# Router's weights loaded first, last feed-forward's norms ahead of its products, last layer's pairs of spread values in one buffer and placed together

## The chip, the cores and the metric

The kernel runs on one core of a Trainium2 chip. The metric is the device time of one execution in microseconds (us). TensorE (PE in the profile), VectorE (DVE), ScalarE (ACT), GpSimd (POOL) and the DMA queues issued by SyncE (SP) and POOL each take their instructions strictly in the order that the program gives them.

## What is computed

A residual stream x of 4 batches x 1024 tokens x 128 channels (f32) passes four layers. Each is a half feed-forward, an attention of some kind, and the same half feed-forward again. The norms have no weights.

```python
x = x + 0.5 * moe0(ln(x));  x = x + attn0(ln(x));  x = x + 0.5 * moe0(ln(x))      # 8 experts, top 2, gelu
x = x + 0.5 * ffn1(ln(x));  x = x + attn1(ln(x));  x = x + 0.5 * ffn1(ln(x))      # silu-gated; 16 heads of 8, rotary
x = x + 0.5 * moe2(ln(x));  x = x + attn2(ln(x));  x = x + 0.5 * moe2(ln(x))      # 8 experts, relu; linear attention
x = x + 0.5 * ffn3(ln(x));  x = x + attn3(ln(x));  x = x + 0.5 * ffn3(ln(x))
# attn3 (16 heads of 8), by token t:   y = r_t . (S + u * k_t v_t);   S = S * exp(-exp(w_t)) + k_t v_t
```

## The kernel before, in words

Channels are the partitions, so the residual of a batch is one 128 x 1024 tile X. All products are f32; a matmul of this type is two PE instructions, so x2 in the trace is one matmul. Nearly all of them go through the helper `mm` (L231).

**Order of the work.** The code states tasks, and a scheduler fixes each engine's order when the program is built, by priority (order of statement, unless raised) and by its own estimate of when operands and buffers are free. `lanes` states several tasks side by side: each task yields its estimated cost, and the lane with the lowest clock goes on. In layer 1's attention PE's order is written out by hand. A pool hands out buffers by tag; a new tile in a buffer waits until the old one has been read.

**Start.** `run` loads constants c0 and the four X tiles by SP's queue, then the weights named in `needs`: l0s (the router, 128 x 8), l0a (attention 0), l1f (whose integers VectorE converts at L604), then those of later layers. `run` multiplies the router's weights by a centring matrix and puts them beside that matrix in `both`, so that one matmul of X with `both` gives the centred tokens and their router logits. `layer0` then centres attention 0's q, k, v weights (`centered`, L263: one matmul, one copy on ScalarE). `route` (L306 to L432) takes squares of the centred tokens on ScalarE, norms them, and ranks, counts and places the tokens; `experts` (L450 to L483) then goes through blocks of 128 slots: fetch an expert's weights, gather tokens, two products, scatter. `combine` (L508 to L517) adds the results to X.

**Layer 1's attention** (`l1_attn`). `prepare(b)` norms a batch, makes q and k with their rotation (L712, L715, summed on POOL at L717) and v (L723); `spread` moves heads by DMA (L731) and POOL (L732) to where the products read them. The loop goes through 256 units; in each, `greatest` (products, then maxima at L744 on VectorE) runs 11 units ahead of `scores` (exponentials at L767 on ScalarE) and `values`. Layer 1's first feed-forward of batch 3 is late: `feed` does it in two halves of 512 tokens, each of 8 steps (centre and square L825, variance L833, scaling L839, three gate/up products L844 and L847, a pause, output), and one step is taken at each yield of `prepare(0)` from the third on, then one in each unit of the loop. ScalarE's square root, exponential and silu are in different tables, whose change is an ACT_TABLE_LOAD.

**Layer 3** (`layer3`). For batches (0, 1) and then (2, 3), two halves of 512 tokens each: `l3_ffn`, `l3_prepare`, `l3_recur`, `l3_finish`, `l3_ffn`, 8 units in all, in five lanes: recurrences, two lanes of finishing work, two of preparing work. The recurrence keeps state element (head, k) by partition and goes through the 8 value columns j in 4 pairs. For each pair two matmuls (tile `wave`, via `together`, L1079) spread the value rows over the partitions; they read different groups of 32 rows (32*128 in the trace). VectorE multiplies by k (`kv`, L1170), scans with the decay (`st`, L1177) and multiplies by r (`z`, L1184; the second of a pair does this on POOL). After two pairs, four matmuls (tile `acc`, also L1079) sum z over the partitions; the first set is stated after the third pair. `l3_prepare` has two pairs of mixing matmuls per unit that go through `together` as well (tile `bank` in L1079). `together` states the matmuls last to first, and a dependency without a semaphore keeps that order on PE; it does not keep other matmuls out from between:

```python
        for out, lhsT, rhs, start, stop in reversed(matmuls):
            i = self.nc.tensor.matmul(out, lhsT, rhs, start=start, stop=stop).ins
            if after is not None:
                self.tc.add_manual_dep(i, after.name, order, reason="side by side")
            after = i
```

Each `wave` tile is 128 x 512 f32, and its pool holds two of them.

Of the kernel before, what the change touches and what calls it, by code (L numbers as in the profile page):

```python
# [17 lines left out]
P = 128  # L18
B, S, D = 4, 1024, 128
# [3 lines left out]
HALF = 512  # L23
# [186 lines left out]
class Macaron:  # L210
# [449 lines left out]
    def l1_attn(self, m, c1, f):  # L660
# [6 lines left out]
        with ExitStack() as ctx:  # L667
            enter = ctx.enter_context
# [186 lines left out]
            late = [feed(b, hf) for b in self.late for hf in range(2)]  # L855
            for n, _ in enumerate(prepare(0)):
                if late and n >= 2:
                    next(late[0], None)
            for z in va:
                nc.gpsimd.memset(z, 0.0)  # L860
                nc.gpsimd.memset(z[:, :, :, 0:1], 1.0)
# [212 lines left out]

    def together(self, matmuls, after=None):

        order = mybir.DependencyInfo(mybir.DependencyClass.NoSync, mybir.DependencyReason.DATA)
        for out, lhsT, rhs, start, stop in reversed(matmuls):
            i = self.nc.tensor.matmul(out, lhsT, rhs, start=start, stop=stop).ins  # L1079
            if after is not None:  # L1080
                self.tc.add_manual_dep(i, after.name, order, reason="side by side")
            after = i
        return after
# [65 lines left out]
    def l3_recur(self, wave, ps, wp, c3, b, h, carries, given):  # L1149
        nc = self.nc  # L1150
        v, pool = nc.vector, nc.gpsimd
        wdec, k, vals, r, y = (given[x] for x in ("wdec", "k", "vals", "r", "y"))
        acc = self.t(ps, [P, HALF], "acc")
        carry = carries[b] if h else self.t(wp, [P, HD], f"carry{b % 2}")
        carries[b] = carry
        held = []
        for w in range(2):
            zs = []
            for pair in range(2):
                js = [4 * w + 2 * pair + i for i in range(2)]  # L1160
                vb = [self.t(wave, [P, HALF], "wave") for _ in js]
                rows = [slice(32 * (j % 4), 32 * (j % 4) + 32) for j in js]
                last = self.together([(vb[i], c3["vrows"][rows[i], w, :], vals[rows[i], :], True, True) for i in range(2)])
                for sums in held:
                    self.together(sums, last)
                held = []
                kv = []
                for i in range(2):
                    kv.append(self.t(wp, [P, HALF], "kv", bufs=3))
                    v.tensor_tensor(kv[i], k, vb[i], ALU.mult)  # L1170
                for i, j in enumerate(js):
                    st = self.t(wp, [P, HALF + 1], "st", bufs=3)
                    if h == 0:
                        v.memset(st[:, 0:1], 0.0)
                    else:
                        nc.scalar.copy(st[:, 0:1], carry[:, j : j + 1])
                    v.tensor_tensor_scan(  # L1177
                        st[:, 1:], wdec, kv[i], carry[:, j : j + 1] if h else 0.0, ALU.mult, ALU.add
                    )
                    if h == 0:  # L1180
                        nc.scalar.copy(carry[:, j : j + 1], st[:, HALF:])

                    z = self.t(wp, [P, HALF], "z", bufs=6)
                    (pool if i else v).tensor_tensor(z, st[:, 0:HALF], r, ALU.mult)  # L1184
                    zs.append(z)
                yield 4.7
            held.append([(acc[32 * q : 32 * q + 32, :], c3["sums"][:, w, :], zs[q], w == 0, w == 1) for q in range(4)])
        for sums in held:
            self.together(sums)
        v.tensor_tensor(y, y, acc, ALU.add)  # L1190
        yield 1
# [33 lines left out]
    def layer3(self, f, t, c3):  # L1225
        sb = lambda name, bufs=2, **k: self.tc.tile_pool(name=name, bufs=bufs, reuse_waits="tile", **k)
        with ExitStack() as ctx:
            enter = ctx.enter_context
            wave, accs, tail, prep = (
                enter(self.psum(name, n)) for name, n in (("l3wave", 2), ("l3acc", 1), ("l3tail", 2), ("l3prep", 3))  # L1230
            )

            tmp, *front = (enter(sb(name, side="right")) for name in ("l3tmp", "l3even", "l3odd"))
            rec, *end = (enter(sb(name)) for name in ("l3rec", "l3ends0", "l3ends1"))
            given, carries, seen = {}, {}, {}
            start = lambda f, *a: lambda: f(*a)
            units = [(b + i, h) for b in range(0, B, 2) for h in range(2) for i in range(2)]
            fronts, recs, ends = ([], []), [], ([], [])
            for b, h in units:
                u = f"{b}{h}"  # L1240
                mine = given[b, h] = {}
                wp, wend = front[b % 2], end[b % 2]
                s = [seen.setdefault((b, i), {}) for i in range(3)]
                fronts[b % 2].extend([
                    (f"ffn{u}0", (), start(self.l3_ffn, prep, tmp, wp, f, b, h, s[0])),
                    (f"prepare{u}", (), start(self.l3_prepare, prep, tmp, wp, t, c3, b, h, s[1], mine)),
                ])
                recs.append((f"recur{u}", (f"prepare{u}",), start(self.l3_recur, wave, accs, rec, c3, b, h, carries, mine)))
                ends[b % 2].extend([
                    (f"finish{u}", (f"recur{u}",), start(self.l3_finish, tail, wend, t, c3, b, h, mine)),  # L1250
                    (f"ffn{u}1", (), start(self.l3_ffn, tail, tmp, wend, f, b, h, s[2])),
                ])
            self.lanes(recs, *ends, *fronts)
# [47 lines left out]
        self.lanes(blocks, back, *more(route))  # L1301

    def layer0(self, moe, m, right, enter, ffn):
        m["wqkvc"] = self.centered(m["wqkv"], 3 * D)
        early = right.enter_context(ExitStack())
        pa, pf = enter(early, "l0a"), enter(right, "l1f0", side="left")
        side, main = self.side, self.main
        self.late = [B - 1]

        def swap():  # L1310

            early.close()
            self.l1_rings(enter(self.rings, "l1rings", 1))
            yield 0

        def more(route):
            attn = lambda b, *after: (f"middle{b}", after, lambda: self.l0_attn(side, pa, m, b))
            last = lambda b, ps: (f"last{b}", (f"combine1{b}",), ffn(pf, ps, b))
            return (
                [  # L1320
                    route(0, (0,), ps=main), route(0, (1,)), route(0, (2, 3)),
                    *[attn(b, f"combine0{b}") for b in range(B)],
                    ("swap", (), swap), *[last(b, side) for b in range(B) if b not in self.late],
                ],
                [route(1, (0, 1), "middle0", "middle1", "combine03"), route(1, (2,), "middle2"), route(1, (3,), "middle3")],
            )


        groups = [(0,), (1,), (2, 3)], [(0, 1), (2,), (3,)]
        marks = {(0, (0,)): "_1", (0, (1,)): "_2", (0, (2, 3)): "_0", (1, (0, 1)): "_0", (1, (2,)): "_1", (1, (3,)): "_2"}  # L1330
        self.macaron("l0", moe, AF.Gelu, groups, marks, more)
# [30 lines left out]
    def run(self, stages):  # L1362
        nc = self.nc
        self.X, self.ring, self.rings, self.late = [], {}, ExitStack(), []
        self.c0 = self.load("c0")
        for b in range(B):
            X = self.t(self.res, [P, S], f"x{b}")
# [9 lines left out]
            "l3": ("l3f", "l3a", "c3"),  # L1377
        }
        tags = {"l1a": "attn_w", "l3a": "attn_w", "c1": "attn_c", "c2": "attn_c", "c3": "attn_c"}
        have = {}  # L1380

        def weights(name):
            if name not in have:
                have[name] = self.l1_weights() if name == "l1f" else self.load(name, tag=tags.get(name))
            return have[name]

        sb = lambda name, bufs=2, **k: self.tc.tile_pool(name=name, bufs=bufs, reuse_waits="tile", **k)
        for n, name in enumerate(stages):
# [3 lines left out]
            if name in ("l0", "l2"):  # L1392
                with self.psum("main", 4) as self.main, self.psum("side", 4) as self.side, sb(name + "moe") as self.fp:
# [4 lines left out]
                    with ExitStack() as right:  # L1398
                        enter = lambda stack, name, bufs=2, side="right": stack.enter_context(sb(name, bufs, side=side))
                        m = dict(weights(name + "a"))  # L1400
# [55 lines left out]
```

## Time and profile before

| | |
|---|---|
| median of 3 runs | 3086.77 us (3083.92 to 3097.02) |
| the profiled execution | 3084.05 us, its span 3082.3 us |
| busy share of the span | PE 87%, DVE 59%, ACT 53%, POOL 26% |
| mean granted TensorE clock | 0.925 |
| layer 0, 0 to 849 us | PE 607 us busy, DVE 542, ACT 488, clock 0.84 |
| layer 1's attention, 849 to 1935 us | PE 1060 us busy, DVE 713, ACT 608, clock 0.99 |
| layer 1's second feed-forward and layer 2, 1935 to 2601 us | PE 584 us busy, DVE 325, ACT 329, clock 0.94 |
| layer 3, 2601 to 3082 us | PE 427 us busy, DVE 252, ACT 202, clock 0.90 |

The boundaries are read from the trace: the first square of layer 1's attention follows 849 us, its last copy of outputs starts at 1932, and layer 3's first norm follows the last combine at 2601. A clock of 1 is full speed. A wait shown in brackets behind a timeline row is the time for which the engine stood idle before it, with what released it. Each L number is a line of the kernel before.

### The profile page before, as it was taken

The numbers are of one execution on the slowest core, as the hardware profiler recorded it, in microseconds if no ns is written. First come the engines' busy times: TensorE is split into PE (matmuls) and PEld (weight loads), VectorE is DVE, ScalarE is ACT, GpSimd is POOL, SyncE is SP. The second block draws the span as 40 slices with busy tenths as digits, with TensorE's granted clock in tenths as the row PEclk, the third lists the DMA queues.
The fourth block names the chain that finished last, engine by engine and source line by source line (L and its number), as shares of the span: only waits on it lengthen the run. The fifth ranks groups of instructions, "written<-read, shape, count | busy, mean of one in ns | idle before, by whom it ended". The sixth has DMA issues, their size and how long they took to land. (4 is left out here: it accounts for less than half of the span.)

```text
span 3082.3 us, 47513 instructions
## 1 busy us (share of the span) xinstructions
PE 2677.2 (87%) x17694; PEld 1544.9 (50%) x17694; DVE 1832.5 (59%) x3215; ACT 1626.7 (53%) x3633; POOL 788.3 (26%) x732
## 2 busy tenths in 40 slices
PE   5868537778989999999999999989898987899997
PEld 5756416665643333333333333568787975343432
DVE  3586886774256776676677774362566632447554
ACT  4655425657725665566565666455454554353532
POOL 4666307553400000000000000037444563001010
PEclk8988768889989999999999999989998998899988
DMA  7766416563500000000000000048665784000000
GB/s 240 225 178 191 120 53 184 169 197 117 164 15 5 5 7 4 5 6 5 19 5 6 1 1 1 21 141 283 199 181 181 219 277 148 1 1 1 7 7 14
DMA packets 122887, 277.63 MB, mean 90 GB/s; under 512 B 18017, under 2 KB 67297, under 8 KB 122529
## 3 DMA queue, kind: packets, MB, share of 16 engines
q1 hardware_dynamic: 101792, 231.83, 24.3%
q0 software_dynamic: 20864, 42.77, 4.9%
q8 instruction: 140, 2.29, 0.3%
q14 instruction: 91, 0.74, 0.1%
HBM read 238.48 MB, written 31.85 MB: 88 GB/s over the span
## 5 line engine op out<-in xcount | busy, mean ns | idle before, releaser
L744 DVE TENSOR_REDUCE nm<-two 128x2 f32<-128x1024 f32 x512 | 626.2, 1224 | 276.1 <-PE s L231 265.1
L767 ACT ACTIVATE e<-s 128x512 f32<-128x512 f32 x1024 | 555.9, 594 | 400.6 <-PE s L231 397.5
L471 ACT ACTIVATE e_h<-bank,e_w 128x128 f32<-128x128 f32 x1304 | 450.3, 368 | 395.7 <-PE bank L231 383.9
L231 PE MATMUL s<-qm,kz 32*128 32x512 f32 x2048 | 631.8, 640 | 0.8 <-ACT e L767 0.8
L231 PE MATMUL bank<-e_x,e_w 128*128 128x128 f32 x2608 | 536.0, 309 | 91.1 <-ACT e_h L471 52.8
L231 PE MATMUL two<-kz,qz 32*128 32x512 f32 x2048 | 576.6, 645 | 20.6 <-DVE nm L744 4.2
L457 POOL DMA_INDIRECT e_xg<-rows,g_source x326 | 343.1, 1052 | 758.5 <-DVE g_l L317 349.9
L231 PEld LDWEIGHTS bank<-e_x,e_w 128*128 128x128 f32 x2608 | 409.1, 202 | 172.7 <-ACT e_h L471 97.6
L231 PE MATMUL bank<-e_w,e_h 128*128 128x128 f32 x2608 | 459.3, 292 | 20.9 <-ACT e_h L471 12.7
L483 POOL DMA_INDIRECT res<-e_y,g_target x326 | 360.4, 1105 | 255.7 <-DVE e_y L482 113.9
L231 PEld LDWEIGHTS bank<-e_w,e_h 128*128 128x128 f32 x2608 | 378.4, 202 | 44.3 <-ACT e_h L471 26.2
L231 PE MATMUL o<-e,va 128*32 128x256 f32 x4096 | 327.4, 391 | 0.1
L231 PEld LDWEIGHTS o<-e,va 128*32 128x32 f32 x4096 | 80.9, 108 | 387.9 <-issue 367.9
L231 PEld LDWEIGHTS two<-kz,qz 32*128 32x128 f32 x2048 | 153.8, 184 | 227.7 <-issue 162.7
L231 PEld LDWEIGHTS s<-qm,kz 32*128 32x128 f32 x2048 | 206.6, 183 | 11.3 <-issue 7.7
L463 DVE COPY e_x<-bank 128x128 f32<-128x128 f32 x326 | 92.7, 285 | 190.1 <-PE bank L461 170.2
L482 DVE TENSOR_TENSOR e_y<-bank,e_w 128x128 f32<-128x128 f32 x326 | 93.9, 288 | 187.6 <-PE bank L231 176.2
L732 POOL COPY va<-vd 128x256 f32<-128x256 f32 x16 | 6.7, 433 | 624.6 <-PE o L231 537.9
L1184 POOL TENSOR_TENSOR z<-st,r 128x512 f32<-128x512 f32 x32 | 46.4, 1449 | 414.2 <-DVE st L1177 343.6
L461 PE MATMUL bank<-c,e_xg 128*128 128x128 f32 x326 | 95.4, 295 | 46.2 <-DMA e_xg<-rows,g_source 39.7
L471 ACT ACT_TABLE_LOAD x53 | 68.0, 1283 | 28.4 <-PE bank L231 18.3
L461 PEld LDWEIGHTS bank<-c,e_xg 128*128 128x128 f32 x326 | 49.5, 152 | 52.4 <-DMA e_xg<-rows,g_source 36.0
(325 smaller groups left out, 3440.1 us busy)
## 6 DMA issues: line engine op xcount, KB each, us to landing
e_w<-in_l0m_dram SPq DMA_DIRECT2D x170, 578.0 KB
e_w<-in_l2m_dram SPq DMA_DIRECT2D x156, 578.0 KB
c_y<-res SPq DMA_DIRECT2D x32, 512.0 KB
rows<-g_xt SPq DMA_DIRECT2D x16, 512.0 KB
e_xg<-rows,g_source POOLq DMA_INDIRECT x326
res<-e_y,g_target POOLq DMA_INDIRECT x326
x<-in_x_dram SPq DMA_DIRECT2D x4, 512.0 KB
qz<-qd SPq DMA_DIRECT2D x64, 32.0 KB
```

What stands on the lines that cost most here:

```text
L231: self.nc.tensor.matmul(out, lhsT, rhs, start=start, stop=stop)
L457: nc.gpsimd.indirect_dma_start(out=xg, out_offset=None, in_=rows[:, :], in_offset=at(source[:, k : k + 1]))
L461: nc.tensor.transpose(tp, xg, self.c0["ident"])
L463: nc.vector.tensor_copy(x, tp)
L471: nc.scalar.activation(h[:, fc, :], o[:, fc, :], func, bias=w[:, 2 * FC * P + fc : 2 * FC * P + fc + 1])
L482: nc.vector.tensor_tensor(y, o, w[:, MOE_W - D :], ALU.add)
L483: ins = nc.gpsimd.indirect_dma_start(out=res[:, :], out_offset=at(target[:, k : k + 1]), in_=y, in_offset=None)
L732: nc.gpsimd.tensor_copy(va[n % RING][:, :, :, 1 : 1 + HD], dense[b, "vd"][:, :, 32 * g4 : 32 * g4 + 32].rearrange("p t (h d) -> p t h d", ...
L744: v.tensor_reduce(nm[:, it, h, 2 * pair : 2 * pair + 2], s, AX.X, ALU.max, negate=True)
L767: nc.scalar.activation(es[g], s, AF.Exp, scale=scale)
L1184: (pool if i else v).tensor_tensor(z, st[:, 0:HALF], r, ALU.mult)
```

## The change

- `run` loads l0s before c0 and the X tiles; it is no longer the sixth load of SP's queue but the first.
- `layer0` no longer centres q, k, v weights ahead of everything; this is a task `center` in a lane, behind the first route.
- `l1_attn` takes the two late halves' first three steps in turns (norm of one, norm of the other), at yields 2 to 7 of `prepare(0)`; from then on the first half goes on with its products, then the second.
- `together` states all but the first of its matmuls at high priority.
- `l3_recur` takes one tile of 128 x 2 x 512 for a pair instead of two of 128 x 512; the pool holds one of it instead of two of the old ones, so the memory is the same.

```diff
@@ l1_attn
             for n, _ in enumerate(prepare(0)):
                 if late and n >= 2:
-                    next(late[0], None)
+                    next(late[n % 2 if n < 8 else 0], None)
@@ together
-        for out, lhsT, rhs, start, stop in reversed(matmuls):
-            i = self.nc.tensor.matmul(out, lhsT, rhs, start=start, stop=stop).ins
+        for n, (out, lhsT, rhs, start, stop) in enumerate(reversed(matmuls)):
+            with self.tc.high_priority() if n else ExitStack():
+                i = self.nc.tensor.matmul(out, lhsT, rhs, start=start, stop=stop).ins
@@ l3_recur
-                vb = [self.t(wave, [P, HALF], "wave") for _ in js]
+                both = self.t(wave, [P, 2, HALF], "wave")
+                vb = [both[:, i, :] for i in range(2)]
@@ layer3
-                enter(self.psum(name, n)) for name, n in (("l3wave", 2), ("l3acc", 1), ("l3tail", 2), ("l3prep", 3))
+                enter(self.psum(name, n)) for name, n in (("l3wave", 1), ("l3acc", 1), ("l3tail", 2), ("l3prep", 3))
@@ layer0
-        m["wqkvc"] = self.centered(m["wqkv"], 3 * D)
...
+        def center():
+            m["wqkvc"] = self.centered(m["wqkv"], 3 * D)
+            yield 0
...
-                    route(0, (0,), ps=main), route(0, (1,)), route(0, (2, 3)),
+                    route(0, (0,), ps=main), ("center", (), center), route(0, (1,)), route(0, (2, 3)),
@@ run
+        have = {"l0s": self.load("l0s")} if "l0" in stages else {}
         self.c0 = self.load("c0")
...
-        have = {}
```

## The prediction

> **What bounds the kernel now.** I read the stretches of the four layers first (engine busy time, granted TensorE clock), then the PE timeline of the last layer, then the starts of layers 0 and 1, and the instruction order of both programs on every engine. The two orders differ in three places only: the first 117 us, the first 45 us of layer 1's attention, and all of layer 3. Between them each engine gets the same instructions in the same order, so a gain or loss made in one place is carried unchanged to the end.
>
> ```profile
> core 0: us, PE busy (x) PEld busy (x) DVE busy (x) ACT busy (x) POOL busy (x), PEclk, DMA share, GB/s
> ...
> 2601.00:3082.30 481.30, 426.71 (x1329) 177.66 (x1328) 252.13 (x395) 202.32 (x356) 46.36 (x32) 0.90 0.01 5
> 2660.00:3040.00 380.00, 353.36 (x1098) 145.98 (x1097) 227.49 (x349) 164.88 (x297) 45.10 (x31) 0.90 0.01 3
> 2990.00:3020.00 30.00, 27.61 (x64) 10.26 (x64) 19.54 (x27) 6.96 (x16) 4.33 (x3) 0.54 0.00 0
> ```
>
> In layer 3 between 2660 and 3040 PE is busy 93% of the time, VectorE 60%, ScalarE 43%, and no DMA works: the order of PE's instructions is what ends the stage. In some stretches (the last line) PE is busy and its clock is about half.
>
> **Layer 3, the pairs of spread values (L1079 `wave`).** Each of 8 recurrence units spreads values in 4 pairs, 32 in all; the two matmuls of a pair use different groups of 32 rows. These lines of the PE timeline show the price of standing apart (x2 is one matmul, x4 is two):
>
> ```profile
> 2721.60 1.12 PE L1079 MATMUL wave<-vals,attn_c 32*128 32x512 f32 x2
> 2722.78 1.12 PE L231 MATMUL bank<-x,c 128*128 128x512 f32 x2
> 2723.83 1.12 PE L1079 MATMUL wave<-vals,attn_c 32*128 32x512 f32 x2
> ```
> ```profile
> 2782.52 1.13 PE L1079 MATMUL wave<-vals,attn_c 32*128 32x512 f32 x4
> 2783.58 0.70 PE L231 MATMUL bank<-x,c 128*128 128x512 f32 x1
> ```
>
> A lone half occupies PE until the next starts: 1.18 us (2721.60 to 2722.78). A whole pair takes 1.06 us (2782.52 to 2783.58). Joining a split pair removes one slot, 1.05 us at full clock. At half clock a lone half took 2.0 us (2961.74 to 2963.74). In the order of before 15 of the 32 pairs are split; in the order of after none is. Of the 15, nine stand at full clock (9 x 1.05 = 9.5), four at half on both sides (2842 to 2847, 2958 to 2962, 2993 to 2997, 3001 to 3007: 4 x 2.0 = 8), two half and half (2 x 1.4 = 2.8): 20.3 us of PE time. By PE's share of 93%, **18.9 us** of it is on the path. The four mixing pairs that are apart in before (L1079 `bank`) stay apart in after and give nothing.
>
> One buffer for two adds no matmul and no copy, and no new kind of wait: the half that is issued first was already the one whose buffer is read last, so a pair waited for the second product of the pair ahead (L1170) then as now. Both halves now wait at one point, and everything behind on PE waits with them. The next pair can start 1.06 + 2 x 0.68 = 2.4 us after the last one was issued; with one joined pair's 1.06 us in between, at most 1.4 us of PE is lost where nothing else stands between. In the order of after that is one place (pairs 26 and 27), and two more have a single matmul between: **+2 us**.
>
> The sums (L1079 `acc`) wait for z from POOL, and this wait is PE's largest in the stage:
>
> ```profile
> 2677.49 1.51 PE L1079 MATMUL acc<-z,attn_c 128*32 128x512 f32 x8 [2.84 <-POOL z L1184]
> ```
>
> In after most sums have 4 to 10 more matmuls ahead of them. The list of waits puts 16.6 us of PE's idle time on it, in nine places. I take **-6 us** off, and give **+3** back for the sums of units 7 to 14, where pairs 26 to 29 come closer together: VectorE needs 2 x 0.68 + 2 x 1.24 + 0.77 = 4.6 us for each pair (rows L1170, L1177, L1184), then POOL 1.45. The bounds of this term are -16.6 (all of it goes) and +10 (seven late pairs, each 1.4 us short).
>
> At the end of the stage the recurrence moves ahead of the finishing work: after the last sums 56 matmuls remain instead of 40. The 16 that move are one finish and part of an ffn (y to the residual took 9.7 us, 3056.4 to 3066.1, in the undisturbed last unit, the rest 3.5 us); they leave the stretch before the last sums and lengthen the one behind, which was 39.4 us (3042.9 to 3082.3). Taken as **0**, bounds -8 and +13. ScalarE keeps its 54 table loads here. Layer 3: -18.9 + 2 - 6 + 3 = **-20 us**.
>
> The clock is the term no row can price in advance. From 2841 to 2862, 2957 to 2974 and 2991 to 3019, 66 us, PE runs at about half and so loses up to 33 us; some 11 us of that is in the lone halves above. I take no more; bounds: -20 (these stretches fill with full-width matmuls and the clock returns), +20 (40 us more at half).
>
> A page of the Trainium skill speaks against counting on this: "TensorE: Matmul & The Clock Gate" (What's actually happening) has the clock set by how busy PE has lately been, full after one busy window of about 3.4 us. The row 2990:3020 differs: busy 27.61 of 30 us and a clock of 0.54. By the page those stretches would be at full clock anyway, each split pair would cost 1.05 us, and layer 3's sum would be -14.6 + 2 - 6 + 3 = -16, inside my range.
>
> **Layer 1's start.** Batch 3's last feed-forward runs beside the first attention preparation. Before, its first half ran whole (norm, three products, output) inside the preparation and its second half beside the first maxima; now both norms come first. What leaves the loop are two table loads, Sqrt at 890 and Silu behind it:
>
> ```profile
> 890.18 1.28 ACT L833 ACT_TABLE_LOAD   x1
> 893.57 1.28 ACT L844 ACT_TABLE_LOAD   x1
> ```
>
> 2 x 1.28 us on ScalarE, hidden already: ScalarE is idle around them (10.07 us before 889.56). What counts is PE's queue ahead of the first maxima. The chain there is q, k products, rotation, kd on POOL (875.42 to 877.77), its DMAs (issued from 877.80), first maxima 880.4. Ahead of the second k product before: three gate/up pairs (3 x 1.72), one norm. After: two norms and one gate/up pair; the other products and the output follow. That takes 2 x 1.72 us off it and puts three norm groups on (1.09, 1.00, 1.06), with a copy (0.69) and a scaling (0.68) on VectorE. But q also stood behind the first gate/up pair, for which PE idled 1.02 us: it ran at 863.6, 2.5 us after its own input was ready (861.1). I take **-3**, bounds 0 and -4. In the loop, three norm matmul groups go (2.0 + 2.0 + 1.1 us as they ran) and one output (2.7 at full clock, 4.7 at half) and the copy-back come: 0, bounds -4 and +5, since the clock is half there from 882 to 893 and 909 to 917. SP's queue and POOL's keep their order.
>
> **Layer 0's start.** The router's 4 KB load passes five loads on SP's queue. PE's first matmul waited for it:
>
> ```profile
> 11.57 0.56 PE L231 MATMUL bank<-l0s,c 128*128 128x8 f32 x2 [11.57 <-DMA l0s<-in_l0s_dram]
> ...
> 14.42 0.28 ACT L306 ACTIVATE g_xt<-bank 128x128 f32<-128x128 f32 x1 [0.23 <-DVE l1f_wd L604]
> ```
>
> After, it waits for the constants (VectorE had them at 4.41) and x0 (landed by 7.41, when SP's load behind it was let go), so three router matmuls run some 5 us earlier. But the centring of wqkv still stands fourth on PE and ahead of the first square on ScalarE, and l0a lands at about 12; and the first square waits for the conversion of l1f (L604), which sits in memory that its tile takes over. Both hide the gain. What is left are gaps of about 1 us between the first squares: **-1 us**. Bounds: -5 (the whole shift), +1.2 (the load's issue took SP 1.22 us and now delays all others). The second route's matmuls move back by one expert block, beside the first experts, whose combine starts at 116.7 us. The five loads queued on semaphores behind wait for one transfer earlier, which nobody is waiting for.
>
> **Sum.** -1 - 3 - 20 = -24 us against the profiled execution (3084.05 us; its span 3082.3): 3060. The median shown is 2.7 us above that execution, so I say **3063**.
>
> **Rivals.** (a) VectorE takes over. A pair delivered 1 us sooner is no use if the 4.6 us of products, scans and z behind it are late. For: pairs 26 to 32 stand within 11 matmuls, 32 us of VectorE work; VectorE's longest waits are for ScalarE's norms (40.6 us), not for `wave` (26.5). Against: 60% busy. Then only joins outside the clusters count, 8 x 1.05 x 0.93 = 8, with 4 from layers 0 and 1: 3075. The Trainium skill, "TensorEngine Tiling (Array Packing)" (PSUM Bottleneck), has this as a rule: tiling speeds up TensorE, not the emptying of PSUM. The row 2660:3040 (VectorE 227 of 380 us) does not show it as the bound yet.
> (b) More than forecast: the sums' waits and the half-clock stretches both go. -24 - 10 - 12: 3041.
> (c) Slower: PE stands still more often in front of joined pairs, and the clock falls after each. At 2689.45 PE idled 2.84 us and then ran at half until about 2698: 2.8 + 4.3 = 7 us. There are 31 pairs behind another; 4 such events more eat the forecast's 24 us, and 6 give 3063 + 42 = 3105, over 0.5% slower. It would show in layer 3's clock below 0.85. Against: only three places with at most one matmul between pairs.
> That the pairs are not placed together is excluded by the order of after.
>
> **How the numbers follow.** Forecast 0.55, (a) 0.20, (b) 0.17, (c) 0.08. The range 3041 to 3081 takes in (a), (b) and the bounds on the near side; what is out is (c) and the far ends. A measurement tells about 0.5%, 15 us, from no change: faster than 3071 is the forecast's bulk and (b), 0.69; within it (a) and the forecast's edge, 0.23; slower 0.08.
>
> **What would show it.** Right: 32 `wave` groups of x4, layer 3 at about 460 us, `acc` waits on POOL below 10 us, first maxima at about 876, first experts' gather 1 us earlier, layer 2 unchanged in length. Wrong: layer 3 within 8 us of 481 with VectorE's `kv` and `mix` waits as long as now (a); clock in layer 3 below 0.85 (c).

## The result, and the profile after

| | before | after |
|---|---|---|
| median | 3083.92 us (5 runs, 3082.16 to 3097.02) | 3059.78 us (5 runs, 3052.73 to 3069.43) |
| ratio, 95% interval | | 0.9912 [0.9894, 0.9929] |
| profiled execution, its span | 3084.05, 3082.3 us | 3069.43, 3067.7 us |
| layer 3, from its first square | 479.4 us | 454.6 us |

The change makes the kernel 0.9% faster; 3063 was predicted. The profiled execution of after is the slowest of its five, 10 us above their median. The 24.8 us gained in layer 3 stand against 10 us lost ahead of it: layer 3 begins at 2613.1 instead of 2602.9. From layer 1's first exponentials to layer 3 both kernels have the same instruction order, and at these exponentials after is only 0.8 us late (928.3 against 927.6). So some 9 of those 10 us belong to this execution and not to the change; "again" below starts layer 3 at 2599.7. The total of -24 was forecast and came (3083.92 to 3059.78), but by other parts than forecast: layer 3 gave some 5 us more than its -20, and the 4 us of the two starts cannot be seen.

In rows of after and of later runs, L numbers are lines of that run's kernel: L1081 there is L1079 of before, L1187 is L1184, L1173 is L1170.

Engine busy time and granted clock by stretch, in after: all of layer 3, from the first to the last pair of spread values, and 30 us before the last sums.

```profile
2612.00:3067.70 455.70, 395.10 (x1328) 168.61 (x1326) 252.32 (x395) 202.38 (x356) 47.00 (x32) 0.93 0.01 5
2671.00:3013.00 342.00, 310.87 (x1078) 128.89 (x1077) 227.44 (x347) 160.24 (x289) 46.78 (x32) 0.97 0.01 4
2981.00:3011.00 30.00, 24.00 (x73) 9.21 (x72) 24.95 (x33) 8.71 (x21) 7.43 (x5) 0.77 0.00 1
```

The first number after the length is PE's busy time: 395 us in layer 3, where before had 427. VectorE, ScalarE and POOL have the same work as before. The clock rose from 0.90 to 0.93, and its middle part runs at 0.97. Where no pair is split, the PE timeline of after shows the two halves as one entry of four instructions between full-width products:

```profile
2782.63 1.02 PE L231 MATMUL bank<-x,c 128*128 128x512 f32 x2
2783.58 1.13 PE L1081 MATMUL wave<-vals,attn_c 32*128 32x512 f32 x4
2784.82 1.16 PE L231 MATMUL bank<-c,n_sq 128*128 128x128 f32 x8
```

The PE rows of the list of waits in layer 3 (us in total, places, longest) have the sums' wait for POOL at half of what it was, first before, then three rows of after:

```profile
PE acc L1079 <- POOL z L1184: 16.6, 9, 2.8
```
```profile
PE bank L231 <- DVE n_r L1010: 9.0, 11, 1.3
PE acc L1081 <- POOL z L1187: 8.3, 7, 1.9
PE bank L231 <- ACT n_sq L1002: 8.0, 10, 2.0
```

**The clock, in steps.** The trace gives the granted clock as stretches at 1 or at 0.5, each a multiple of 3.41 us; a half step below is a step of 3.41 us at half clock. Here are eight such steps of before, around one of the half-clock stretches of the prediction:

```profile
2951.05:2954.46 3.41, 3.14 (x16) 1.49 (x14) 3.41 (x5) 0.19 (x1) 0.00 (x0) 1.00 0.38 154
2954.46:2957.88 3.42, 1.09 (x9) 0.26 (x9) 3.42 (x6) 0.19 (x1) 1.54 (x1) 1.00 0.00 0
2957.88:2961.29 3.41, 3.41 (x4) 0.85 (x4) 2.40 (x4) 0.38 (x2) 0.87 (x1) 0.50 0.00 0
2961.29:2964.70 3.41, 3.41 (x4) 1.00 (x4) 2.14 (x4) 0.00 (x0) 0.40 (x1) 0.50 0.00 0
2964.70:2968.12 3.42, 3.42 (x5) 0.87 (x4) 3.31 (x6) 2.25 (x6) 0.53 (x1) 0.50 0.00 0
2968.12:2971.53 3.41, 3.41 (x9) 1.68 (x9) 0.52 (x1) 2.82 (x4) 1.01 (x1) 0.50 0.00 0
2971.53:2974.94 3.41, 3.41 (x13) 1.01 (x13) 1.66 (x4) 2.18 (x3) 0.00 (x0) 0.50 0.00 0
2974.94:2978.36 3.42, 3.42 (x9) 1.43 (x8) 0.00 (x0) 0.76 (x2) 0.00 (x0) 1.00 0.00 0
```

In the second row PE works only 1.09 us; the next five rows are at half. What stopped it, and what it ran at half clock, is in the PE timeline:

```profile
2956.79 1.06 PE L1079 MATMUL acc<-z,attn_c 128*32 128x512 f32 x8 [2.60 <-POOL z L1184]
2957.78 2.02 PE L1079 MATMUL wave<-vals,attn_c 32*128 32x512 f32 x2
2959.73 2.08 PE L231 MATMUL bank<-t,wo_lng 128*128 128x512 f32 x2
2961.74 2.07 PE L1079 MATMUL wave<-vals,attn_c 32*128 32x512 f32 x2
```

A wait of 2.60 us at the sums, and then lone halves in turn with full products: half clock for 17 us, though PE never stands still. Summed over layer 3, before has 88.7 us of half steps in ten stretches, after 58.0 in eight, the first of which began in layer 2 (whole steps are counted). PE's streaming in them (the time in which columns run through the array, from the starts and sizes of the matmuls) is 73.0 and 46.2 us, of which half is lost: 36.5 and 23.1. On PE's own account the clock is 13.4 us. What that is worth at the end is an estimate: among eight executions, four of the old order and four of the new (before, starts_only, l0_only, l1_only; after, again, l3_only, no_l1), one us more at half clock goes with 0.35 us more of layer 3 (0.40 among the old, 0.23 among the new), so that 30.7 us fewer are worth 10.7, give or take 2. So of the 24.8 us gained **some 9 to 13 are the clock**, 12 to 16 the rest.

### The profile page after: what moved, and what is told of

It reads as the page before. It is cut to its first block, busy times and chain, and to the rows that moved or that the text cites. A ratio compares the mean times of both kernels' runs of the same rounds, so it can differ in the third digit from the quotient of the medians.

```text
span 3067.7 us, 47519 instructions
## 1 busy us (share of the span) xinstructions
PE 2661.9 (87%) x17694; PEld 1542.5 (50%) x17694; DVE 1833.5 (60%) x3215; ACT 1624.4 (53%) x3631; POOL 788.2 (26%) x732
## 5 line engine op out<-in xcount | busy, mean ns | idle before, releaser
L1187 POOL TENSOR_TENSOR z<-st,r 128x512 f32<-128x512 f32 x32 | 47.0, 1469 | 373.7 <-DVE st L1180 260.2
L471 ACT ACT_TABLE_LOAD x53 | 68.0, 1283 | 28.3 <-PE bank L231 18.3
```

The lines of the kernel that those rows point to most:

```text
L471: nc.scalar.activation(h[:, fc, :], o[:, fc, :], func, bias=w[:, 2 * FC * P + fc : 2 * FC * P + fc + 1])
```

## The experiments

The first eight ran on a chip where before takes 3219.69 and 3225.92 us (medians of 23 runs for each four kernels), the last four on one where it takes 3091.83. Ratios are against before on the same chip. On the first chip and in the two first profiles, layer 3 with the old order of pairs takes 479 to 487 us with 89 to 109 us at half clock, and with all pairs joined 454 to 455 with 48 to 58. On the last chip only the joined order was traced as it stands ("again": 451 us, 48 at half). It lies within 4 us of the others, so lengths of layer 3 are set side by side.

### Which part of the change brings the gain

`l3_only`: before with both edits of layer 3.

```diff
+            with self.tc.high_priority() if n else ExitStack():
...
+                both = self.t(wave, [P, 2, HALF], "wave")
...
+("l3wave", 1)
```

> The kernel before with layer 3's part of the change alone (one buffer for a pair, its halves placed together); layers 0 and 1 start as before. All 32 pairs of spread values stand together, as in the changed kernel. Theory S (split pairs cost PE slots on the path): layer 3 lasts about 455 us instead of 479, total 20 to 25 us shorter, ratio 0.992 to 0.994. Rival T (the starts of layers 0 and 1 bring the gain): ratio 0.998 or more.

`priority_only`: the first line of that alone, in `together`.

> The kernel before with high priority in the helper that places matmuls side by side, and nothing else; a pair keeps two buffers. One pair is still split instead of 15, and 55 matmuls follow the last sums as in the changed kernel. Theory S: about the whole of layer 3's gain, layer 3 at 453 to 462 us, ratio 0.992 to 0.995. Rival B (the single buffer is what brings the gain): layer 3 at 475 us or more, ratio 0.998 or more.

`buffer_only`: the other two alone, one tile for a pair.

> The kernel before with one buffer for both halves of a pair, and nothing else. 14 pairs are still split. Theory S: layer 3 within 6 us of 479, ratio 0.998 to 1.002. Rival B: layer 3 at 460 us or less, ratio 0.994 or less.

`starts_only`: after with layer 3 as in before.

```diff
-            with self.tc.high_priority() if n else ExitStack():
...
+                vb = [self.t(wave, [P, HALF], "wave") for _ in js]
```

> The changed kernel with layer 3 as before: only the router's weights first, the centring in a lane and the norms of the late feed-forward first. My prediction had 4 us for this (1 + 3): ratio 0.9987. The trace of the changed kernel speaks for less: first gather 0.2 us later than before, first maxima 4 us earlier, but the twelfth unit of layer 1's loop not earlier at all; by it the ratio is 1.000. Rival T: ratio 0.994.

| | ratio, 95% interval | pairs split | layer 3, us | at half clock, us |
|---|---|---|---|---|
| l3_only | 0.9920 [0.9901, 0.9938] | 0 | 455.0 | 58.0 |
| priority_only | 0.9931 [0.9911, 0.9950] | 1 | 458.6 | 64.9 |
| buffer_only | 1.0018 [1.0002, 1.0035] | 14 | 486.0 | 95.6 |
| starts_only | 1.0028 [1.0010, 1.0045] | 15 | 480.2 | 92.2 |

The gain is layer 3's, and the high priority joins the pairs; one buffer without it leaves 14 split and gains nothing. Its layer 3 is just outside the 6 us expected, but no longer than where layer 3 is untouched (486.7 and 486.3 us in l0_only and l1_only below). Rivals T and B fall. The loss in starts_only was expected by neither theory. The high priority holds for all that goes through `together`, sums and mixing matmuls too, so these runs do not part joined pairs from the rest of the new order; `serial` below bears on that.

### The two starts by themselves

`l0_only` and `l1_only` make one start's edits to before; `no_l1` is after without layer 1's.

```diff
+        have = {"l0s": self.load("l0s")} if "l0" in stages else {}
...
+                    route(0, (0,), ps=main), ("center", (), center), route(0, (1,)), route(0, (2, 3)),
```

> The kernel before with layer 0's two edits alone (router's weights loaded first, centring of q, k, v weights behind the first route). Both starts together measured 1.0028 [1.001, 1.0045]. Theory H (the loss is half-clock windows at the start of layer 1, where the trace shows 10 us more of them and the first exponentials 1.8 us later): about 1.000 here, within +-0.001. Rival L (layer 0's new order costs the rest): 1.002 or more, and a first stretch (up to the first square of layer 1) that is 4 to 9 us longer than in the kernels with the old start.

```diff
+                    next(late[n % 2 if n < 8 else 0], None)
```

> The kernel before with layer 1's edit alone (both late norms first). Theory H: first maxima 4 us earlier after the first square, but first exponentials 1.5 to 2 us later and 7 to 10 us more at half clock between them: ratio 1.0006. My prediction's own value was -3 us, ratio 0.999. Rival L expects 1.000 to 1.0006 as well, and the rest of the measured loss in layer 0.

```diff
-                    next(late[n % 2 if n < 8 else 0], None)
+                    next(late[0], None)
```

> The kernel after without layer 1's edit: layer 0's start, joined pairs. Theory H: as good as the change of layer 3 alone, 0.992, and 2 us better than the whole change. Rival L: 0.994, since layer 0's loss of some 7 us stays.

l0_only 0.9993 [0.9973, 1.0012], l1_only 1.0008 [0.9989, 1.0027], no_l1 0.9907 [0.9888, 0.9927]. Rival L falls. The product of the first two, 1.0001, does not repeat the 1.0028 of both. Before itself differs between the two sets of runs on this chip by 0.2% (3219.69 and 3225.92), which no ratio within one set shows: starts_only's median of 3226.12 is no loss against the second. What the starts cost together is open by some 0.3%, and neither is a gain that can be told. From the first square of layer 1 to its first exponentials, where layer 1's edit acts, all 13 traces line up when the time at half clock beside it is read:

| | length, us | at half clock, us |
|---|---|---|
| old order (7 traces) | 75.4, 76.4, 76.5, 78.2, 78.3, 78.4, 78.9 | 16.3, 18.2, 18.3, 22.8, 23.0, 23.1, 24.2 |
| new order (6 traces) | 76.2, 76.8, 79.0, 80.0, 80.1, 80.5 | 24.6, 25.9, 30.7, 32.0, 33.1, 33.6 |

At 24.6 us of half clock the new order takes 76.2 us, at 24.2 the old one 78.9: 2.7 us less, and the maxima do begin 3 us earlier after the first square. But it has 9 us more at half clock on average (30.0 against 20.8), at nearly half a microsecond each, and ends 1.3 us later (78.8 against 77.4). The PE timeline shows where: both late outputs (`l1f_wd`) now fall into half-clock steps, 5.1 and 5.3 us for six instructions, of which before's first took 2.7. The first row is before, the others after.

```profile
873.92 2.74 PE L231 MATMUL s<-e,l1f_wd 128*128 128x512 f32 x6
```
```profile
876.29 5.06 PE L231 MATMUL two<-kz,qz 32*128 32x512 f32 x12 [1.12 <-POOL va L732]
881.53 2.08 PE L231 MATMUL two<-kz,qz 32*128 32x512 f32 x4 [0.19 <-DVE nm L744]
883.54 5.12 PE L231 MATMUL s<-e,l1f_wd 128*128 128x512 f32 x6
...
903.67 5.29 PE L231 MATMUL s<-e,l1f_wd 128*128 128x512 f32 x6
```

### What sets the clock

`clock` leaves out all layers and lets PE run stretches written out by hand: stalls of nine lengths among full products, then a stall and one of four mixes, then halves alone.

```diff
+            for columns in STALLS:
+                for _ in range(6):
+                    stall(columns)
+                    dense(18)
+            for kind, n in ((dense, 14), (lone, 8), (pairs, 8), (alone, 12)):
+                for _ in range(5):
+                    stall((HALF,) * 4)
+                    kind(n)
+                    dense(16)
+            for _ in range(3):
+                alone(30)
+                dense(16)
```

> A kernel that leaves out all four layers (its output is its input) and lets PE run hand-ordered stretches. From the traces I read the rule C: the clock is set anew every 3.41 us; it halves where the window before was streaming less than some 0.4 of its time, and comes back only after a window that streamed over 0.85 of it. First part: nine lengths of stall, six times each, between 18 full-width products. C: stalls up to 1.5 us never bring a half window, 2.1 to 4.1 us bring one in some of the six by where they fall, none below 2. Second part: a stall of about 4 us, then one of four mixes, five times each. C: full-width products return to full clock after 1 window; lone 32-row halves in turn with full products stay at half for 2 windows or more, and so do 32-row halves alone; joined pairs with full products 1 to 2. Third part: 30 lone 32-row halves without a stall keep the full clock (share 0.72, above 0.4). The rival, that the clock is full again one busy window after any stall, expects 1 window in all four mixes.

None of the 54 stalls of the first part, the longest 1.71 us, brought a half step. The stall ahead of each mix was 2.17 us, not 4 as expected. Behind full products it brought one half step in three of five cases, namely where a single step held at least 2.2 us without streaming, and none where the gap was shared and no step held over 1.9. With lone halves in turn with full products the half clock lasted 11, 9, 10, 10 and 10 steps, until the mix ended; with the same products in joined pairs 3, 2, 1, 2 and 0; with twelve halves and nothing else (the fourth mix) 4, 7, 7, 4 and 7. The two PE rows below are the same 64 instructions (8 halves, 24 full products), split and joined; the windows are the half clock behind the stall of each, and the full clock that follows in the second.

```profile
1172.56 47.88 PE L232 MATMUL bank<-x,c 32*128 32x512 f32 x64
```
```profile
1426.84 30.64 PE L232 MATMUL bank<-x,c 32*128 32x512 f32 x64
```
```profile
1171.10:1208.60 37.50, 37.50 (x39) 10.01 (x38) 0.00 (x0) 0.00 (x0) 0.50 0.00 0
1427.10:1437.30 10.20, 10.20 (x16) 2.92 (x14) 0.00 (x0) 0.00 (x0) 0.50 0.00 0
1437.30:1455.00 17.70, 17.70 (x45) 7.27 (x44) 0.00 (x0) 0.00 (x0) 1.00 0.00 0
1782.10:1826.40 44.30, 44.30 (x53) 17.03 (x52) 0.00 (x0) 0.00 (x0) 0.50 0.00 0
```

The rival, one busy window after any stall, falls. So does the last part of C: the fourth window is the third part, 30 lone halves with no stall, and they fell to half clock by themselves for 13 steps (13 and 14 in the other two). Busy time is not what counts. Weighing each matmul's streaming time (0.427 us per instruction of 512 columns at full clock) by rows/128 and columns/128 gives a measure that fits: from full clock PE falls to half behind a step with less than 0.37 of it, and comes back behind one with more than about 0.75. In the trace of before this misses 2 of 762 steps at full clock and 3 of 135 at half (its own best second limit is 0.73), in `clock` 0 of 441 and 1 of 130, in after none at full clock and 11 of 135 at half. The plain share of time in which PE streams, with the limits that fit it best, misses 10 and 20 in `clock`. Only the weight of the rows is shown: all products of `clock` are 128 columns wide, and in the traces of the kernel the measure without the columns fits about as well.

### The same orders with other products

`serial`: after with both halves of a pair on the same 32 rows. `full_rows`: after with each half as a product over 128 rows. `before_full`: the same in before.

```diff
-... c3["vrows"][rows[i], w, :], vals[rows[i], :], True, True) ...
+... c3["vrows"][rows[0], w, :], vals[rows[0], :], True, True) ...
```

> The kernel after, every engine's order unchanged, but both halves of a pair read the same group of 32 rows, so that they can't run side by side (this computes other value columns than the reference). Both theories: each pair takes some 2.0 us of PE in place of 1.06, 32 x 0.98 x 0.93 = 29 us more. Theory U (the clock follows how much of the array works: streaming time x rows/128 x columns/128 over a window of 3.41 us, half below about 0.37, full again above about 0.75): 85 us or more of layer 3 at half clock in place of 58, layer 3 at 497 us or more in place of 454.7. Rival N (PE's idle time alone makes half windows): 58 us at half, layer 3 at 484.

```diff
-... c3["vrows"][rows[i], w, :], vals[rows[i], :], True, True) ...
+... c3["vfull"][:, js[i] % 4, w, :], vals, True, True) ...
```

> The kernel after, every engine's order unchanged, but each half is a product over all 128 rows with a matrix that is zero outside its 32 (same result; POOL builds the matrices early). A pair is then two full products, 1.72 us in place of 1.06: 32 x 0.66 x 0.93 = 20 us more PE time in both theories. Theory U: such a product counts four times as much, so at most 40 us of layer 3 at half clock in place of 58, layer 3 at about 467 us. Rival N: 58 us at half, 475 us.

The edit of `before_full` is the same line.

> The kernel before, every engine's order unchanged, 15 pairs still split, with each half a product over all 128 rows as in full_rows. PE time by the slots: 17 whole pairs x (1.72 - 1.06) - 30 lone halves x (1.18 - 0.86) = +1.6 us. Theory U: less than 60 us of layer 3 at half clock in place of 90, layer 3 at about 468 us in place of 479.4, with nothing joined. Rival N: 90 us at half, 481 us.

`again` is after, unchanged.

> The kernel after itself, on the chip of these runs. If layer 3 brings all of the gain and both starts nothing that can be told: 0.991 to 0.993, with layer 3 at 454.7 us and 58 us of it at half clock. If the 1.0028 measured for the starts alone were theirs: 0.995.

| | layer 3, us | PE busy, us | PE not busy, us | at half clock, us |
|---|---|---|---|---|
| before | 479.4 | 424.8 | 54.6 | 88.7 |
| before_full | 469.3 | 412.7 | 56.6 | 51.2 |
| after | 454.6 | 394.1 | 60.5 | 58.0 |
| again | 451.4 | 389.7 | 61.7 | 47.8 |
| full_rows | 461.4 | 409.7 | 51.7 | 41.0 |
| serial | 467.8 | 421.3 | 46.5 | 61.4 |

again: 0.9915 [0.9896, 0.9935] of before as a whole; no_l1 with 0.9907 cannot be told from it, so no version is better than the change.

before_full is as theory U had it (468 us, below 60 at half): no pair is joined, no engine's order changed, and layer 3 is 10 us shorter than before's, and shorter than all four traces with 15 split pairs (479.4 to 486.7). The expectations named theory U, the measure above, and rival N, PE's idle time alone, which `clock` had already against it: the 30 halves had no stall. Layer 3 of before in three parts and the same parts of before_full, by the list of windows:

```profile
2602.90:2842.00 239.10, 214.33 (x713) 91.96 (x712) 124.30 (x196) 111.47 (x196) 20.02 (x14) 0.96 0.00 0
2842.00:2988.00 146.00, 139.49 (x408) 56.02 (x404) 80.95 (x129) 64.00 (x108) 14.85 (x11) 0.88 0.02 8
2988.00:3082.30 94.30, 70.98 (x211) 29.35 (x210) 46.13 (x64) 26.85 (x52) 11.50 (x8) 0.81 0.03 11
```
```profile
2596.50:2836.00 239.50, 220.43 (x689) 98.14 (x690) 118.13 (x187) 111.24 (x194) 18.50 (x13) 0.94 0.00 0
2836.00:2977.00 141.00, 129.92 (x425) 57.19 (x424) 86.10 (x136) 63.95 (x110) 16.11 (x11) 0.98 0.02 8
2977.00:3065.80 88.80, 62.37 (x215) 28.67 (x213) 48.08 (x65) 27.46 (x53) 11.76 (x8) 0.92 0.03 12
```

The first part is equal, the gain is in the two where the clock rose (0.88 to 0.98, 0.81 to 0.92). Two things act at once there, which this run does not part: wider products count more, and they take longer, so that the wait of 2.60 us at the sums is 1.87 in before_full. Shorter waits are not the whole of it: the sums' waits are 17.8 us in eleven places there, not less than before's 16.6. full_rows also lies on U's side (41 us at half), though faster than both expected.

serial missed both expectations, though its time at half clock (61.4) is near N's 58. PE's busy time rose by 27.2 us as worked out (29), but its idle time fell by 14.0, and layer 3 grew by 13.2; the time at half clock hardly rose. U's 85 us did not come. The measure itself holds in this trace (5 of 767 steps at full clock missed, 4 of 128 at half); what went wrong is that the 85 us were reckoned with PE's waits as they are in after. The second slot of a pair fills waits at the sums, 3.3 us in place of 8.3; that these would have started half steps is not shown. full_rows says the same with 15.6 us of busy time and 6.8 of length, both with 17 us less at half clock in them. Against again instead of after the two ratios are 16.4 of 31.6 and 10.0 of 20.0. So a microsecond of PE work added beside the recurrence was worth 0.44 to 0.52 us at the end, not 0.93.

serial also says that side by side is not all of the gain. The two rows are one of its pairs, 1.91 us until the next row's matmul begins, and its wait at the sums:

```profile
2779.33 1.98 PE L1081 MATMUL wave<-vals,attn_c 32*128 32x512 f32 x4
```
```profile
PE acc L1081 <- POOL z L1187: 3.3, 3, 1.5
```

None of its 32 pairs runs side by side, where 17 did in before, and PE is busy nearly as long (421.3 against 424.8 us). Still its layer 3 is 11.6 us shorter than before's, with 8.1 us less idle time and 27 us less at half clock. So the new order has a worth of its own, through the waits at the sums and the clock; how much of the 24.8 us is that and how much the slots was not parted.

## Why the prediction was right

**Layer 3, the sum.** -20 was predicted, -24.8 measured (-24 to -35 between single traces of the two orders): the place was right, and so was the edit that brings it, the high priority that joins the pairs, as l3_only and priority_only show. That the gain is the saved slots is only half of the account, and the terms were mis-sized:

- *Split pairs, 18.9 us by "PE's share of 93%".* The slots were there: PE's busy time fell by 30.7 us, the clock's part included. The share was lower: over the whole change 24.8 of 30.7, 0.81, because PE's idle time rose by 5.9 us (waits for norms and ScalarE's tiles grew). For work added to the new order, serial and full_rows measure 0.44 to 0.52; no run removes slots alone. As an estimate, the 15.75 us of slots at full clock are then worth between 7.4 (at 0.47) and 12.8 us (at 0.81), where 0.93 gives 14.6.
- *"The clock is the term no row can price in advance", taken as 0 beyond some 4 us inside the lone halves.* It brought some 9 to 13. This is the step that failed, though its bound of -20 holds it: the rows of before already showed what comes together there. Of the four stretches in the three places named, two (2841 and 2957) began at a wait of the sums for POOL, one right behind (2855) another, the last (2992) at a wait of 2.13 us for ScalarE, and lone halves ran in them; the change acts on both. The list also left out eight half steps, 27 us, elsewhere in the layer. The two errors, a clock taken some 5 to 9 us too small and slots taken 2 to 7 us too large, go against each other, so that the sum is partly luck.
- *Sums' waits, -6 and +3.* The PE rows show -8.3 (16.6 to 8.3), while other waits of PE grew. The wait itself can be the small part of its price: six of the nine in before were followed by one to five half steps, 3 to 17 us.
- *+2 for joined pairs, 0 for the end of the stage.* The waits of `wave` for VectorE are 3.0 us in five places in after (1.6 in two before), and the last sums are at 3013.6, 54 us before the end as against 39 in before; the end of the stage is longer by what moved there, as taken. ScalarE's table loads are 56 in both, not 54.

**The rule of the Trainium skill.** The Trainium skill, "TensorE: Matmul & The Clock Gate" (What's actually happening), ties the clock to how busy PE has recently been, with one busy window of about 3.4 us enough for full clock. The traces agree on the length, 3.41 us, and that the window before decides. They differ on both limits. The Trainium skill's section "HAM oscillation — how this bites in real kernels" on the same page warns of idle gaps above some 3.4 us; here waits of 2.17 and 2.60 us were enough. And one busy window did not bring the clock back: in `clock` it took about 0.75 of the array at work, and PE was busy for 37.5 us at half clock without it.

**Layer 1, -3.** Right in PE's work, wrong in time: first maxima at 878.0 in place of 882.1, and 2.7 us less at equal clock, but 9 us more at half clock, +1.3 in all. The order differs up to the second late output, 63 us into the layer in before, and not for 45. The half clock was named in the term of the loop (0, bounds -4 and +5), whose upper bound holds it; taken as 0 it was mis-sized by 4.

**Layer 0, -1.** First router matmul at 5.54 in place of 11.57, as foreseen; the centring stayed at 12.16 and the first square at 14.51 behind L604, as foreseen; first experts' gather 37.17 in place of 36.96, so nothing was gained. Both rows in after:

```profile
5.54 0.56 PE L231 MATMUL bank<-l0s,c 128*128 128x8 f32 x2 [5.54 <-DMA c<-in_c_dram]
```
```profile
14.51 0.28 ACT L306 ACTIVATE g_xt<-bank 128x128 f32<-128x128 f32 x1 [0.19 <-DVE l1f_wd L604]
```

**Rivals.** (a) VectorE did not take over: it is busy 252 of 454.6 us, and PE's waits for `kv` are 3.0 us. (b) came in part: half-clock stretches and sums' waits shrank by more than forecast, but the split slots brought less and the starts nothing that can be told. (c) did not come; layer 3's clock rose.

## What to carry to other kernels

Read the granted clock step by step before pricing PE work: find the wait that begins each half-clock stretch and the narrow products that keep it up, and price both; a wait of 2.6 us was followed by five half steps here. Put products that use different rows side by side, not only because a slot is saved but because a stretch of them keeps the array full enough. Price work on the busiest engine by an experiment or by its waits, not by its busy share: at 93% busy a microsecond added was worth about half of one at the end, and one that the whole change removed 0.81.

## What the hardware showed that was not expected

- The clock has memory: it halves behind a step of 3.41 us with less than about 0.37 of the array's streaming capacity used, and returns only behind one with about 0.75 (no miss in 441 steps and one in 130 of `clock`). Between the two it stays as it is, 9 to 11 steps for lone halves in turn with full products.
- Work counts by the rows of the array that it uses. Products over 32 rows one after the other, with no stall, ran 13 or 14 steps at half clock.
- Products over all 128 rows with zeros in 96 of them, more work on paper, made before 10 us faster in layer 3. As a whole it took 3067.86 us (one run) against 3091.83; what this difference holds beyond those 10 us is not explained.
